# A state tile of four n-parts by 32 channels, and sums that begin with y in PSUM

## The chip, the cores and the metric

The kernel runs on one NeuronCore of one Trainium2 chip. The metric is device time in microseconds; the time before is the median of three runs, 29361.2 us (29357.19 to 29361.32). All data are float32.

## The reference, cut to what matters

The program is four vision layers, one after the other, each of the Mamba kind. Per image (8 of them, 64 x 64 positions, 96 channels) a layer projects to 192 inner channels, convolves, and then scans the positions in K directions (K is 4 in three layers and 1 in the last). For each direction k:

```
x_dbl = einsum('bkdl,kcd->bkcl', xs, x_proj_w)
dts, Bs, Cs = jnp.split(x_dbl, [DT_RANK, DT_RANK + D_STATE], axis=2)
delta = softplus(einsum('bkrl,kdr->bkdl', dts, dt_proj_w) + dt_proj_b)
def step(h, inp):
    dA = jnp.exp(d_t[..., None] * A[None])
    h = dA * h + (d_t * u_t)[..., None] * b_t[:, :, None, :]
    y = jnp.einsum('bkdn,bkn->bkd', h, c_t)
    return (h, y)
ys = scan(step) + Ds * xs
y  = sum of ys over the directions, each put back to its positions
```

With 192 channels d and 16 states n there are 3072 recurrences of 4096 steps for each direction and image. Afterwards y is normalised (in three layers), gated by silu(z), projected to 96 channels and added to x.

## The kernel before, in words

A loop over the 8 images holds the four layers. A layer has a first part (norm, input projection, convolution), the scans, and a last part (norm of y, gates, output projection). The scans take nearly all of the time. They walk over chunks of 512 positions: 8 chunks a direction, in the order of directions 0, 2, 1, 3; directions 2 and 3 run backwards. In all there are 832 chunks.

The work on one chunk, `i`, is cut into 24 *units*; a unit is 128 recurrences over 512 positions. In the kernel before, the 128 partitions of a unit are 2 n-parts by 64 channels (so 3 channel groups t times 8 states j). Four units with the same t make a *state tile* h of 128 x 2048. Six state tiles are a chunk.

For each unit and tile:

- `enter` (matmuls at L942): TensorE forms the input of two units (dbu) in a PSUM tile of two banks. It multiplies du (delta times u, with positions on the partitions, 64 columns of channels) by a block of diagonal matrices with the values of B. 16 products of 64 x 64 weights by 128 columns fill it; each float32 product appears as two records in the trace. There are two such tiles, so TensorE works one tile ahead.
- `decay` (L959): ScalarE forms exp(delta x A) for one unit, four units ahead of the scan. Six buffers.
- `scan` (L973): VectorE runs the recurrence over 512 positions for one unit.
- `keep` (L987): ScalarE copies the last column of the four units as the next chunk's initial state.
- `read_out` (L992): GpSimd multiplies the state tile by C, in place. C stands in SBUF as tiles c of 128 x 2048, two a chunk, each filled by four transfers that repeat rows of DRAM over 64 partitions (`spread_c`, L815). The very last state tile of a layer is done by VectorE (L996).
- `add_up` (L1010): TensorE adds over n with a 0/1 matrix of 64 columns; the sums gather in two PSUM banks (y0 and y1 tiles, `ps_y`).
- `close_sums` (L1019 to L1038): VectorE adds the bank to y in SBUF (L1038), at the places where the direction has its positions; in direction 0 it writes D times u plus the bank (L1032), and ScalarE copies one half (L1036).

The order on every engine is the program's: `tc.manual_schedule` keeps each engine's queue as written. The main loop at L1119 goes over units m; `slot` is m modulo 24 within a chunk. At each m it issues keep and read_out of the tile that was finished (every fourth m), then `enter` for the next pair, `scan(m)`, `decay(m + 4)`, `add_up` (at every fourth slot, for units 15 slots back), and then what the dictionary `plan` (L1041) has for the slot. The plan prepares chunk i + 1, and i + 2:

- v = projection of x_dbl (`turn_v`, L832) at slots 21 and 0; `keep_b` and four steps of softplus on ScalarE at slots 1 to 3; `delta_of` (L877, the sum that ends softplus, on GpSimd) at slot 3.
- `turn_u` (transposes, L849 and L853) at 4 and 5, `du_of` (L880, VectorE) at 7.
- `turn_back` (L898 to L910, delta with the channels back on the partitions) at 8 and 9, and `keep_delta` (L912) at 9, 10, 11: ScalarE copies 64 channels from PSUM into one half of a tile (L917), and a transfer on SP's queue copies them to the other half (L918).
- loads of u (`load_u`, 128 partitions at L749, 64 at L751), x_dbl, `spread_b` and the diagonals (L888, L896), the projection to x_dbl (L765) with `keep_x_dbl` at 18 (L781, then transfers at L790, L792, L794).

All transfers are issued on SP's queue, in the program's order. v, u_t, delta_ps and x_dbl share one PSUM tile of two banks in turn.

Of the kernel before, what the change touches and what calls it, by code (L numbers as in the profile page):

```python
# [30 lines left out]
DI = 192  # L31
NS = 16
NT = 3
NJ = 8
NH = 4
# [10 lines left out]
NEGMEAN, CEN_B, ONE, EPS, N_CONST = 352, 416, 480, 481, 482  # L46
# [73 lines left out]
def kernel(ctx: ExitStack, tc: tile.TileContext, x_in, const_in, *rest):  # L120
# [3 lines left out]
    def pool(name, bufs, space=None):  # L124
# [9 lines left out]
        cpool=pool("c", 3),  # L134
        upool=pool("u", 4),
        deltas=pool("delta", 6),
# [40 lines left out]
def layer(tc, env, x, stats, x_of, x_to, n, ly):  # L177
# [23 lines left out]
    def piece(name):  # L201
        return env.deltas.tile([128, CH], F32, tag="delta", name=name)
# [12 lines left out]
    d = env.wts.tile([128, 2], F32, tag="d", name=f"d{n}")  # L215

    def fold():
        of = win_x[:, 0:by_pe].unsqueeze(1).to_broadcast([C, ly.taps, by_pe])
        nc.vector.tensor_tensor(taps, taps, of, ALU.mult)  # L219

        for o, np_ in enumerate((128, 64)):
            at = ly.d + o * K
            nc.vector.tensor_reduce(
                d[0:np_, o : o + 1], w[0:np_, at : at + K], mybir.AxisListType.X, ALU.add
            )

# [156 lines left out]
    def two_banks(name):  # L383
# [3 lines left out]
        tc, env, n, ly, w, u_mem, u_chunk, d, neg_a, make_ys, two_banks, wide  # L387
# [144 lines left out]
    with set_of("natural_log_exp_and_others"):  # L532
# [15 lines left out]
        env.cpool.tile([128, 4, CH], F32, tag="c", name="gates"),  # L548
# [147 lines left out]
def scans(tc, env, n, ly, w, u_mem, u_first, d, neg_a, make_ys, two_banks, wide):  # L696
# [9 lines left out]
    sel = const[:, SEL : SEL + 64]  # L706
# [3 lines left out]
    RS, SL = 6, 24  # L710
    halves = [slice(0, 64), slice(64, 128)]
# [14 lines left out]

    def place(s):

        i, r = divmod(s, RS)
        return i, r // NT, r % NT  # L730
# [7 lines left out]
    def u_of(i, half):  # L738
        return u_first(half, 0) if i == 0 else us[i][0 : (128, 64)[half], half, :]

    def load_u(i, part):
        if i >= len(walk):
            return
        k, c = walk[i]
        if part == 0:
            us[i] = env.upool.tile([128, 2, CH], F32, tag="u", name="u")
        s = slice(c * CH, (c + 1) * CH)
        if part == 0:
            nc.sync.dma_start(us[i][:, 0, :], u_mem[k % 2][0:128, s])  # L749
        else:  # L750
            nc.sync.dma_start(us[i][halves[part - 1], 1, :], u_mem[k % 2][128:DI, s])  # L751

    def project(i, half):
# [8 lines left out]
        for e in range(2):  # L762
            rows = slice(0, 128) if half == 0 else halves[e if i > 1 else 0]
            u = u_first(half, walk[i][1]) if i < 2 else us[i][rows, half, :]
# [8 lines left out]
    def keep_x_dbl(i):  # L773
# [14 lines left out]
        if i > 1:  # L788
            there = env.deltas.tile([128, CH], F32, tag="delta", name="x_hi")[64 : 64 + XP]
# [17 lines left out]
    def spread_c(i, g, part):  # L807
        k, c = walk[i]
        if part == 0:
            cs[i, g] = env.cpool.tile([128, NH, CH], F32, tag="c", name="c")  # L810
        half, pair = divmod(part, 2)
        rows, js = slice(64 * half, 64 * half + 64), slice(2 * pair, 2 * pair + 2)
        n0 = half * NJ + g * NH + 2 * pair
        of = c_mem[k][n0 : n0 + 2, c * CH : (c + 1) * CH]
        nc.sync.dma_start(cs[i, g][rows, js], of.partition_broadcast(64))  # L815
# [5 lines left out]
    def turn_v(i, b):  # L821


        if b == 0:
            for name in ("delta_t", "du_t"):
                turned[i, name] = env.turned.tile([128, NB4, DI], F32, tag=name, name=name)
# [13 lines left out]
    def turn_u(i, b, half):  # L840
# [5 lines left out]
        for b_ in (b, 2 + b):  # L846
# [3 lines left out]
            else:  # L850
                at = halves[b_ // 2 if i > 0 else 0]
                u = us[i][at, 1, :] if i > 0 else u_of(i, 1)
                nc.tensor.transpose(to[:, 128:DI], block(b_, u), ident[at, at])  # L853

    def softplus(i, part):

        v = turned[i, "v"][:, :, 0:DI]
        if part == 0:
            rests[i] = env.turned.tile([128, NB4, DI], F32, tag="rest", name="rest", bufs=1)
# [38 lines left out]
    def turn_back(i, o, part):  # L898
# [3 lines left out]
        for b in (2 * part, 2 * part + 1):  # L902
            of = turned[i, "delta_t"][:, b]
            for half in range(o + 1 if i == 0 else 1):
                to = deltas[i, "ps"][64 * half : 64 * half + 128 // (o + 1), o]
                of_ = of[:, 0:128] if o == 0 else of[:, 128:DI]
                if half == 0:
                    nc.tensor.transpose(block(b, to), of_, ident)  # L908
                else:
                    nc.tensor.matmul(block(b, to), of_, ident, start=True, stop=True)  # L910

    def keep_delta(i, t):  # L912

        delta = env.deltas.tile([128, CH], F32, tag="delta", name="delta")
        if i > 0:
            here = halves[t % 2]
            nc.scalar.copy(delta[here], deltas[i, "ps"][here, t // 2])  # L917
            nc.sync.dma_start(delta[halves[1 - t % 2]], delta[here])  # L918
        elif t == 2:
            nc.scalar.copy(delta, deltas[i, "ps"][:, 1])  # L920
        else:
            for half in range(2):
                of = deltas[i, "ps"][64 * t : 64 * t + 64, 0]
                nc.scalar.copy(delta[64 * half : 64 * half + 64], of)
        deltas[i, t] = delta


    def enter(q):
# [4 lines left out]
        i, g, t = place(s)  # L933
# [3 lines left out]
        for b in range(NB4):  # L937
            for e in range(2):
                rows = slice(64 * e, 64 * e + 64)
                for half in range(2):  # L940
                    at = b * NS + g * NJ + half * NH + 2 * pair
                    nc.tensor.matmul(  # L942
                        to[64 * half : 64 * half + 64, e, b],
                        du[rows, b, 64 * t : 64 * t + 64],
# [6 lines left out]
    def decay(m):  # L951
# [4 lines left out]
        i, g, t = place(s)  # L956
        d_a = env.decays.tile([128, CH], F32, tag="d_a", name="d_a")
        at = (walk[i][0] * NT + t) * NJ + g * NH + m4
        nc.scalar.activation(d_a, deltas[i, t], AF.Exp, scale=neg_a[:, at : at + 1])  # L959
        decays[m] = d_a  # L960

    def scan(m):
        s, m4 = divmod(m, NH)
        i, g, t = place(s)
# [6 lines left out]
        j = t * NJ + g * NH + m4  # L971
# [268 lines left out]
```

## Time and profile before

| | before |
|---|---|
| median of three runs | 29361.2 us |
| the profiled execution, its own time | 29331.35 us |
| its span | 29329.6 us |
| mean granted TensorE clock | 0.98 |
| VectorE scans, L973 (two groups) | 20778.0 + 2838.3 us busy, 19968 instructions |
| GpSimd products, L992 | 22450.1 us busy, 4960 instructions |
| TensorE dbu, L942 | 11236.9 us busy, 319488 records |
| TensorE sums, L1010 | 9697.2 us busy, 39936 records |
| ScalarE decays, L959 | 13372.2 us busy, 19968 instructions |
| data moved | 3498.19 MB, 119 GB/s |

A group of the page gives the busy time of all its instructions together (overlaps counted once), the mean duration of one, and the idle time of the engine just before them with what ended it. TensorE's records overlap heavily, since different parts of its array work at the same time; for it the time from one group's start to the next in the timeline is the measure, not the duration of one record. A timeline line gives start, length, engine, line, operation and how many instructions were merged; a bracket gives the idle time ahead of it and who ended it.

### The profile page before, as it was taken

To read this page: it belongs to the slowest core of one execution; us is meant where nothing else is said; L and a number is where in the kernel's file an instruction comes from. 1 tells how busy PE (TensorE), PEld (TensorE's weight loads), DVE (VectorE), ACT (ScalarE), POOL (GpSimd) and SP (SyncE) were. 2 spreads that over 40 slices of the span, in tenths; PEclk is the share of its full clock that TensorE was granted. 3 is DMA by queue.
4 is the path that set the end of the run, shared out by engine and by line. 5 is a ranking of instruction groups with operands and counts; after the bars stand their busy time and mean duration, and the time that the engine had idled before them with its cause. 6 is when DMAs were issued, how large, how long until landed. Compare 5 with 4: busy or idle time off the path is not lost. (4 is left out here: it accounts for less than half of the span.)

```text
span 29329.6 us, 919486 instructions
## 1 busy us (share of the span) xinstructions
PE 27127.0 (92%) x391056; PEld 15249.2 (52%) x391056; DVE 27395.8 (93%) x26841; ACT 19839.6 (68%) x35728; POOL 25414.1 (87%) x7101
## 2 busy tenths in 40 slices
PE   9999999999999999999999999999999999999999
PEld 5555455554555545555455554555545555455554
DVE  9999899998999989999899998999989999899998
ACT  6667666676666766667666676666766667666676
POOL 8898788987889878898788987889878898788987
PEclk9999999999999999999999999999999999999999
DMA  5444454454544545445454454544545455454454
GB/s 132 117 117 125 106 131 117 117 125 106 131 116 118 125 107 130 118 118 125 106 132 117 116 126 107 131 117 116 125 106 131 116 117 125 106 132 117 116 126 106
DMA packets 1947780, 3498.19 MB, mean 119 GB/s; under 512 B 448400, under 2 KB 469264, under 8 KB 1920624
## 3 DMA queue, kind: packets, MB, share of 16 engines
q1 hardware_dynamic: 1943664, 3438.91, 47.7%
q8 instruction: 3120, 51.12, 0.8%
q14 instruction: 996, 8.16, 0.1%
HBM read 2787.17 MB, written 302.84 MB: 105 GB/s over the span
## 5 line engine op out<-in xcount | busy, mean ns | idle before, releaser
L992 POOL TENSOR_TENSOR h<-h,c 128x2048 f32<-128x2048 f32 x4960 | 22450.1, 4567 | 44.5 <-ACT state L987 37.6
L973 DVE TENSOR_TENSOR_SCAN h<-d_a,state,dbu 128x512 f32<-128x512 f32 x17472 | 20778.0, 1274 | 13.0 <-PE dbu L942 6.0
L959 ACT ACTIVATE d_a<-delta,neg_a 128x512 f32<-128x512 f32 x19968 | 13372.2, 719 | 428.1 <-DVE h L973 390.9
L942 PE MATMUL dbu<-diag,du_t 64*64 64x128 f32 x319488 | 11236.9, 275 | 1631.8 <-DVE h L973 1606.6
L942 PEld LDWEIGHTS dbu<-diag,du_t 64*64 64x64 f32 x319488 | 8881.1, 131 | 6556.5 <-issue 5591.6
L1010 PE MATMUL y_ps<-h,const 128*64 128x512 f32 x39936 | 9697.2, 605 | 13.3 <-POOL h L992 13.3
L1010 PEld LDWEIGHTS y_ps<-h,const 128*64 128x64 f32 x39936 | 2441.1, 136 | 3802.9 <-issue 3757.3
L987 ACT COPY state<-h 128x4 f32<-128x4 f32 x4992 | 974.6, 195 | 3692.8 <-DVE h L973 3687.3
L973 DVE TENSOR_TENSOR_SCAN h<-d_a,dbu 128x512 f32<-128x512 f32 x2496 | 2838.3, 1201 | 348.9 <-PE dbu L942 227.6
L877 POOL TENSOR_TENSOR delta_t<-delta_t,rest 128x768 f32<-128x768 f32 x832 | 1525.5, 1834 | 1835.3 <-ACT state L987 1508.3
L917 ACT COPY delta<-delta_ps 64x512 f32<-64x512 f32 x2400 | 1392.3, 580 | 1716.2 <-PE delta_ps L908 1677.1
L832 PE MATMUL v<-w,x_dbl 39*128 39x208 f32 (+1 forms) x5120 | 1388.4, 475 | 33.3 <-ACT x_dbl L781 33.3
L480 POOL TENSOR_TENSOR acc<-acc,more 128x512 f32<-128x512 f32 x576 | 757.4, 1317 | 758.0 <-ACT more L479 724.4
L343 PE MATMUL one_bank<-xn,taps 96*128 96x512 f32 (+1 forms) x2496 | 1220.2, 675 | 22.0 <-DVE taps L219 22.0
L832 PEld LDWEIGHTS v<-w,x_dbl 39*128 39x128 f32 (+1 forms) x5120 | 964.1, 317 | 348.4 <-issue 228.9
L880 DVE TENSOR_TENSOR du_t<-delta_t,u_t 128x768 f32<-128x768 f32 x832 | 782.9, 941 | 162.2 <-POOL delta_t L877 162.2
L871 ACT COPY bt<-v 128x64 f32<-128x64 f32 x832 | 176.5, 212 | 1109.7 <-PE v L832 1108.3
L908 PE MATMUL delta_ps<-const,delta_t 128*128 128x128 f32 (+1 forms) x6656 | 925.6, 280 | 0.0
L1038 DVE TENSOR_TENSOR y<-y,y_ps 128x128 f32<-128x128 f32 (+2 forms) x2048 | 843.9, 457 | 52.0 <-PE y_ps L1010 52.0
L621 POOL TENSOR_TENSOR y<-y,rstd 128x512 f32<-128x512 f32 x192 | 244.3, 1273 | 743.6 <-DVE y L624 531.6
L849 PE MATMUL u_t<-const,u 128*128 128x128 f32 x3328 | 850.3, 338 | 0.0
L343 PEld LDWEIGHTS one_bank<-xn,taps 96*128 96x128 f32 (+1 forms) x2496 | 473.7, 205 | 705.4 <-issue 691.5
(109 smaller groups left out, 15376.3 us busy)
## 6 DMA issues: line engine op xcount, KB each, us to landing
c<-cm SPq DMA_DIRECT2D x3584, 256.0 KB
c<-xm SPq DMA_DIRECT2D x3072, 256.0 KB
diag<-rows SPq DMA_DIRECT2D x6656, 64.0 KB
delta<-delta SPq DMA_DIRECT2D x2400, 128.0 KB
u<-u SPq DMA_DIRECT2D x1088, 256.0 KB
u<-u SPq DMA_DIRECT2D x1920, 128.0 KB
u<-u SPq DMA_DIRECT2D x48, 1024.0 KB
x_dbl<-xm SPq DMA_DIRECT2D x512, 78.0 KB
```

What stands on the lines that cost most here:

```text
L343: nc.tensor.matmul(part, taps[:, t, d0 : d0 + nd], rhs, start=t == 0, stop=t == ly.taps - 1)
L832: nc.tensor.matmul(turned[i, "v"][:, 2 * e + b], block(2 * e + b, of), w[o : o + XP, at : at + DI + NS], start=True, stop=True,)
L849: nc.tensor.transpose(to[:, 0:128], block(b_, u_of(i, 0)), ident)
L877: nc.gpsimd.tensor_tensor(delta_t, delta_t, rests.pop(i), ALU.add)
L908: nc.tensor.transpose(block(b, to), of_, ident)
L917: nc.scalar.copy(delta[here], deltas[i, "ps"][here, t // 2])
L942: nc.tensor.matmul(to[64 * half : 64 * half + 64, e, b], du[rows, b, 64 * t : 64 * t + 64], diag[rows, :, at : at + 2], start=True, stop=True,
L959: nc.scalar.activation(d_a, deltas[i, t], AF.Exp, scale=neg_a[:, at : at + 1])
L973: nc.vector.tensor_tensor_scan(hs[s][:, m4, flow], decays.pop(m)[:, flow], p[:, flow], 0.0 if first else states[i // NCH][:, j : j + 1], A ...
L987: nc.scalar.copy(states[i // NCH][:, at : at + NH], hs[s][:, :, last])
L992: nc.gpsimd.tensor_tensor(hs[s], hs[s], cs[i, g], ALU.mult)
L1010: nc.tensor.matmul(sums[i][o][64 * half : 64 * half + 64], sel, hs[of][:, state, :], start=g == 0 and e in (0, 4), stop=g == 1 and e in (3 ...
```

## The change

A unit's 128 partitions become 4 n-parts by 32 channels: six channel groups t times four states j, again 24 units. A state tile holds two t by two j (`groups` gives the order of the six tiles). What follows from it:

- `enter`: 32 products of 64 x 32 weights by 128 columns fill a dbu tile, where 16 of 64 x 64 did; a product's output goes to 32 partitions.
- `add_up`: a 0/1 matrix of 32 columns (`SEL_Q`); four products side by side fill the 128 partitions of a bank.
- delta is needed in all four n-parts. ScalarE copies it from PSUM in two pieces (`keep_delta`), it is written to DRAM, and eight transfers (`spread_delta`) bring it into two tiles of 3 channel groups each, repeated over the four parts.
- C: one tile a chunk, filled by four transfers (repeated over 32 partitions); `read_out` reads it twice, by a repeated row.
- y: `open_sums` begins a bank with a TensorE product: the identity times y so far, or in direction 0 the diagonal of D times u (`diag_d`, made once a layer). `add_up` accumulates onto it, and in `close_sums` ScalarE copies the whole bank to y. VectorE has no part in it any more.
- Buffers: c 2 (3 before), u 3 in two tags (4), delta 4 of 6 KB (6 of 2 KB), one buffer `passing` for the softplus rest, for delta on its way to DRAM and for x_hi. One of the gate tiles of the last part moves from c's buffers to h's.
- The plan: opening at slots 12 and 0, closing at 5 and 13 (11 and 14 before), loads of u at 6, 9, 10 (1, 2, 4 before).

The core of the diff:

```diff
-NT = 3
-NJ = 8
+NQ = 4
+DQ = 32
+NT = DI // DQ
+NJ = NS // NQ
...
-    def keep_delta(i, t):
-
-        delta = env.deltas.tile([128, CH], F32, tag="delta", name="delta")
-        if i > 0:
-            here = halves[t % 2]
-            nc.scalar.copy(delta[here], deltas[i, "ps"][here, t // 2])
-            nc.sync.dma_start(delta[halves[1 - t % 2]], delta[here])
...
+    def keep_delta(i, o):
+
+        if o == 0:
+            deltas[i, "sb"] = passing("delta_sb").rearrange("p (o l) -> p o l", o=2)
+            deltas[i, "mem"] = env.dram.tile([DI, CH], F32, tag="delta", name=f"delta{i}_{n}", bufs=2)
+        rows = slice(0, 128 // (o + 1))
+        nc.scalar.copy(deltas[i, "sb"][rows, o], deltas[i, "ps"][rows, o])
+        at = slice(0, 128) if o == 0 else slice(128, DI)
+        nc.sync.dma_start(deltas[i, "mem"][at], deltas[i, "sb"][rows, o])
+
+    def spread_delta(i, part, q):
+
+        if q == 0:
+            deltas[i, part] = env.deltas.tile([128, 3, CH], F32, tag="delta", name="delta")
+        of = deltas[i, "mem"].rearrange("(t r) l -> r t l", r=DQ)[:, 3 * part : 3 * part + 3]
+        nc.sync.dma_start(deltas[i, part][DQ * q : DQ * q + DQ], of)
...
         for b in range(NB4):
             for e in range(2):
                 rows = slice(64 * e, 64 * e + 64)
-                for half in range(2):
-                    at = b * NS + g * NJ + half * NH + 2 * pair
+                for q_ in range(NQ):
+                    at = b * NS + q_ * NJ + 2 * pair_j
                     nc.tensor.matmul(
-                        to[64 * half : 64 * half + 64, e, b],
-                        du[rows, b, 64 * t : 64 * t + 64],
+                        to[DQ * q_ : DQ * q_ + DQ, e, b],
+                        du[rows, b, at_d : at_d + DQ],
                         diag[rows, :, at : at + 2],
...
-            nc.gpsimd.tensor_tensor(hs[s], hs[s], cs[i, g], ALU.mult)
+            h = hs[s].rearrange("p (t j) l -> p t (j l)", j=2)
+            c = c.rearrange("p j l -> p (j l)").unsqueeze(1).to_broadcast([128, 2, 2 * CH])
+            nc.gpsimd.tensor_tensor(h, h, c, ALU.mult)
...
+    def open_sums(i, o):
+
+        sums[i, o] = env.ps_y.tile([128, CH], F32, tag=f"y{o}", name=f"y{o}_ps")
+        if walk[i][0] == 0:
+            work = [(sums[i, o], us[i, o])]
+        else:
+            work = list(y_pieces(i, o))
+        weights = diag_d[:, o] if walk[i][0] == 0 else ident
+        for at, (to, of) in enumerate(work):
+            nc.tensor.matmul(
+                to, weights, of, start=at == 0, stop=False, skip_group_check=True
+            )
+
+    def close_sums(i, o):
+        for of, there in y_pieces(i, o):
+            nc.scalar.copy(there, of)
...
-        11: [(keep_delta, 1, 2), (close_sums, -1, 0)],
-        14: [(close_sums, -1, 1)],
+        12: [(open_sums, 0, 0)],
+        13: [(close_sums, -1, 1)],
...
-        *((5 + 3 * part, (spread_c, 0, part)) for part in range(4)),
-        *((18 + 3 * part, (spread_c, 1, part)) for part in range(4)),
+        *((12 + q, (spread_delta, 0, q)) for q in range(NQ)),
+        *((17 + q, (spread_delta, 1, q)) for q in range(NQ)),
+        *((8 + 5 * q, (spread_c, q)) for q in range(NQ)),
```

## The prediction

> **What bounds the kernel now.** I first read the page's busy shares: three engines are near full, so shares decide nothing.
>
> ```profile
> PE 27127.0 (92%) x391056; PEld 15249.2 (52%) x391056; DVE 27395.8 (93%) x26841; ACT 19839.6 (68%) x35728; POOL 25414.1 (87%) x7101
> ```
>
> Second, busy time by stretch. Nearly all of the span is scan work, and inside it VectorE has no gap, while TensorE and GpSimd have a few per cent.
>
> ```profile
> 500.00:600.00 100.00, 95.58 (x1516) 55.91 (x1520) 99.83 (x91) 70.31 (x129) 96.06 (x24) 1.00 0.54 128
> ```
>
> Columns: stretch, length, busy us of PE, PEld, DVE, ACT, POOL with counts, TensorE clock, DMA share, GB/s. Third, VectorE's timeline over one chunk (24 scans).
>
> ```profile
> 522.30 0.93 DVE L880 TENSOR_TENSOR du_t<-delta_t,u_t 128x768 f32<-128x768 f32 x1
> 523.14 4.79 DVE L973 TENSOR_TENSOR_SCAN h<-d_a,state,dbu 128x512 f32<-128x512 f32 x4
> 527.84 0.67 DVE L1038 TENSOR_TENSOR y<-y,y_ps 128x512 f32<-128x512 f32 x1
> 528.42 3.63 DVE L973 TENSOR_TENSOR_SCAN h<-d_a,state,dbu 128x512 f32<-128x512 f32 x3
> 531.96 0.67 DVE L1038 TENSOR_TENSOR y<-y,y_ps 128x512 f32<-128x512 f32 x1
> 532.53 20.15 DVE L973 TENSOR_TENSOR_SCAN h<-d_a,state,dbu 128x512 f32<-128x512 f32 x17
> 552.60 0.93 DVE L880 TENSOR_TENSOR du_t<-delta_t,u_t 128x768 f32<-128x768 f32 x1
> ```
>
> From du_t to du_t is 30.30 us: 24 scans at 1.18, the du product at 0.84, two y additions at 0.58 from start to start. Nothing is waited for: VectorE is the bound. GpSimd is next:
>
> ```profile
> 496.32 22.65 POOL L992 TENSOR_TENSOR h<-h,c 128x2048 f32<-128x2048 f32 x5
> 520.18 1.84 POOL L877 TENSOR_TENSOR delta_t<-delta_t,rest 128x768 f32<-128x768 f32 x1 [1.21 <-ACT state L987]
> 521.98 13.61 POOL L992 TENSOR_TENSOR h<-h,c 128x2048 f32<-128x2048 f32 x3
> ```
>
> Six products at 4.53 and one addition at 1.80 make 28.98 us a chunk; its one idle time (1.21) stands ahead of the addition, which waits for ScalarE's softplus. The addition ends at 522.02 and VectorE's du_t starts at 522.30: that handover has 0.28 us to spare. TensorE's timeline:
>
> ```profile
> 518.60 1.12 PE L942 MATMUL dbu<-diag,du_t 64*64 64x128 f32 x32
> 521.05 1.11 PE L942 MATMUL dbu<-diag,du_t 64*64 64x128 f32 x32
> 522.09 1.94 PE L1010 MATMUL y_ps<-h,const 128*64 128x512 f32 x8
> 523.96 1.12 PE L942 MATMUL dbu<-diag,du_t 64*64 64x128 f32 x32
> 525.00 1.09 PE L908 MATMUL delta_ps<-const,delta_t 128*128 128x128 f32 x8
> 526.03 1.11 PE L942 MATMUL dbu<-diag,du_t 64*64 64x128 f32 x32
> ```
>
> A dbu group costs 1.05 us to the next start, an add_up group 1.87. A chunk has 12 and 6 of them: 12.6 + 11.2 us, and 4.7 for the rest (v 2 x 0.73, u_t 1.4, delta_ps 1.03, x_dbl 1.67 in half of the chunks): 28.5 of 30.3.
>
> **The change, part by part.** The sum is made against the profiled execution, 29331.35 us (span 29329.6), which is 0.1% below the median of the runs.
>
> *y leaves VectorE.* L1038 (2048 instructions, 843.9 us) and L1032 (640 in four shapes: 140.9 + 139.9 + 59.4 + 55.5 = 395.7) go: 1239.6 us of busy time. From start to start each takes about 0.09 less than its duration (0.67 against 0.58), so 2688 x 0.09 = 242 comes off: **-1000 us**, all on the bound. A chunk's VectorE time becomes 29.1 us. GpSimd, at 28.98, is 0.1 behind it: the gain ends there, and nothing more could come of VectorE.
>
> *ScalarE copies the bank.* Two copies at about 0.50 from start to start (L917's shape of 512 columns has 0.58 duration), or up to four of 128 to 256 columns a bank in the serpentine layer; one of the three keep_delta copies and the k=0 copy at L1036 go. ScalarE goes from 70 to about 73% and hides it. The copies stand at slots 5 and 13, after ScalarE's rush of softplus (slots 1 to 3) and before its work for delta_ps. Behind each wait decays that run four scans (4.7 us) ahead; the add_up they wait for was issued two slots earlier. Cost 0; without the cover 1.0 a chunk.
>
> *open_sums.* Two 128x128 products by 512 columns a chunk. The nearest row is L343 (128 columns of weights, 512 moving: 1133.0 us for 2112 records, 0.54 each, two records a product): 1.07 each, 2.1 a chunk. The serpentine layer has pieces of 128, by L849's row 0.44 for two, so up to 1.8 a bank. Nothing is waited for: y was written a direction earlier, u a chunk earlier.
>
> *add_up.* The same 48 records a chunk, each now on 32 columns of the array, so four stand beside each other where two did. Bounds: 0.93 us a group if four stream at once, 1.87 if only two do. I take 0.93, as two already start within 0.03 us of each other now.
>
> *dbu: the crux.* 64 records a group where 32 were, of half the weight columns, the same 128 moving. What it costs depends on whether eight tiles stream at once. No row shows eight; the rows of four, in narrow windows (each repeats the whole group so far):
>
> ```profile
> 506.13 0.34 PE L942 MATMUL dbu<-diag,du_t 64*64 64x128 f32 x4 [1.23 <-DVE h L973]
> 506.13 0.45 PE L942 MATMUL dbu<-diag,du_t 64*64 64x128 f32 x8 [1.23 <-DVE h L973]
> 506.13 0.56 PE L942 MATMUL dbu<-diag,du_t 64*64 64x128 f32 x12 [1.23 <-DVE h L973]
> 506.10 0.24 PEld L942 LDWEIGHTS dbu<-diag,du_t 64*64 64x64 f32 x8 [1.44 <-issue]
> ```
>
> Windows: 506.13 to .16, .27 to .33, .376 to .432, and .10 to .25 for the weights. Four matmuls start within 0.03 us, then four more each 0.11 us: a round lasts as long as one tile's stream, and issue uses a quarter to a half of it. Eight rounds of eight then take what eight rounds of four take: 1.05 us. Bounds: 1.05 (eight at once), 2.09 (33 ns a record as now). I take 1.05, since the rounds are paced by the stream. TensorE's chunk is then 12.6 + 5.6 + 2.1 + 4.7 = 25.0 us, under VectorE's 29.1. TensorE becomes the bound from (29.1 - 12.4)/12 = 1.39 us a group, and the kernel slower than before from 1.49.
>
> The Trainium skill speaks against this. "TensorE: Matmul & The Clock Gate", the section "Wait — 56ns, not 53.3ns?", says that matmul starts never come closer than about 25 ns, however few columns. By it a group is 64 x 25 = 1.6 us, a chunk 31.6, the kernel about 30400. "Runtime: NRT & Kernel Launch", section "Instruction fetch mechanics", has a floor of some 20 cycles an instruction, which would be worse. The four starts within 30 ns contradict the first page here; whether 64 can follow each other so, no run here shows.
>
> *delta through memory.* Before: three copies, three transfers of 128 KB between halves (L918). After: two copies, two writes, eight reads of 192 KB for a chunk; SP issues 7 more there, and 4 fewer of c. SP takes 0.5 to 0.6 us an issue (L918 0.51, L815 0.59). First copy at 526.1 by ScalarE's rows, write issued at 526.7, first read after the write's landing. No row gives a landing; the loads of x issued at 1051.18 let POOL L565 start at 1057.42, 6.2 us for two of 768 KB, the upper bound; rows<-bt at 1165.66 lets the diagonals go at 1167.12, 1.5 us, the lower. With 3: reads are issued 530 to 535 among diagonals and c, the last there near 539. Decay 24 wants it at slot 20, about 537.5, its scan comes at 542: a wait on ScalarE that VectorE doesn't see. The second part, behind keep_x_dbl on SP (537.5), ends near 545, for a decay at slot 2 about 546. If late, softplus behind it on ScalarE, then GpSimd's addition, then du_t are, and that handover has 0.28 us. I allow 0.1 to 0.2 us a chunk over 832: **+120 us**; bounds 0 and 1 us a chunk (+830).
>
> *Beside these.* GpSimd's product reads c with a repeated row: I take 4.53 us; bounds 4.5 (the shortest L992) and 4.8 (L480's 1317 ns for 512 columns, times four, would be 5.3, but that holds four starts). Layer ends: add_up is TensorE's tail there (22 records from 1055.24 in 5.4 us); half of three groups, 1.4 us for 32 layers, **-45 us**. Layer starts: 3 copies fewer of 0.58 on ScalarE, against a trip through memory, 0 with 2 us either way, 60 in all. Two diagonals of D per layer: 64 x about 0.3 = **+20 us**. Fewer buffers (c 2, u 3, delta 4): each is refilled after its last reader by at least four slots; 0.
>
> Sum: 29331 - 1000 + 120 - 45 + 20 = 28426; with the 30 us to the median, **28450**, 3.1% faster.
>
> **The rivals.**
> - *TensorE becomes the bound (slower).* More than 1.49 us a dbu group. Halfway between the bounds, at 1.57: chunk 12 x 1.57 + 12.4 = 31.2, +0.9 x 832 = 30150; at 1.65: 32.2, 30900; at 2.09: 37.5, 35300. For: no row with eight tiles, 128 instructions to issue in 1.05 us. Against: the four starts in 0.03 us.
> - *GpSimd takes over.* Its product may grow by 0.02 us without harm; by 0.1, chunk 29.6, 28850; by 0.22 the gain is gone, 29400. For: 96 of 100 us busy; against: same elements, contiguous runs of 1024.
> - *Delta is late.* 0.5 to 1 us a chunk: 28750 to 29150. For: the 0.28 us handover. Against: decays lead by four scans.
> - *The freed time is worth nothing*, another wait filling it to the same time: 29360. VectorE's 99.8% speaks against it.
>
> **How the numbers follow.** Forecast 0.55; TensorE 0.24 (up to 1.65 us a group 0.15, above 0.09); GpSimd 0.09 (0.045 faster, 0.015 the same, 0.03 slower); delta late 0.09; nothing 0.03. Faster 0.55 + 0.09 + 0.045 = 0.68, same 0.03 + 0.015 = 0.05, slower 0.24 + 0.03 = 0.27. By 0.2% a measurement of this kernel can be told from no change. The likeliest case alone lies in 28200 to 28950 (no stall and a better tail; 0.6 us a chunk more). The whole range keeps its lower end and reaches to TensorE at 1.65 us a group: 28200 to 30900; 0.09 lie above, less below.
>
> **What would show it.** Right: du_t to du_t at about 29.1 us, a dbu group of 64 at 1.05 us and add_up at 0.93, GpSimd's idle time before delta_t gone. Wrong: VectorE's scans waiting for dbu with a long group (TensorE), du_t waiting for delta_t (GpSimd or late delta), or d_a waiting for a transfer.

## The result, and the profile after

The changed kernel takes 31935.0 us (median of four runs, 31913.7 to 31973.1) against 29361.3 for the kernel before: 1.0878 times as long, 95% interval 1.0859 to 1.0897. The forecast was 28450, with a range up to 30900. The profiled execution took 31973.06 us, its span is 31971.2, the granted TensorE clock 0.929 (before 0.98).

Page of the changed kernel: the busy line, and the queues with their packets and megabytes.

```profile
PE 27460.2 (86%) x715408; PEld 15417.4 (48%) x715408; DVE 26583.0 (83%) x24217; ACT 19973.2 (62%) x37200; POOL 25543.6 (80%) x7101
...
q1 hardware_dynamic: 2204272, 3887.88, 46.7%
q8 instruction: 5648, 92.54, 1.3%
```

No engine is near full any more. VectorE's busy time fell by 813 us, and its share from 93 to 83%. TensorE has 1.8 times as many records as before (391056), and with them its instruction stream, queue q8, has grown: 92.54 MB in 5648 packets are 16 KB each. For each record there is a weight load, 2 x 715408 instructions in all, so a packet brings about 256 of them, of 64 bytes. The page of before has `q8 instruction: 3120, 51.12, 0.8%`.

One row of the view by stretch, the same stretch as was shown of before (length, then busy us of TensorE, its weight loads, VectorE, ScalarE and GpSimd, then clock, DMA share, GB/s):

```profile
500.00:600.00 100.00, 84.20 (x2453) 49.59 (x2434) 84.84 (x74) 59.59 (x112) 87.20 (x21) 0.91 0.52 130
```

VectorE had 99.83 of 100 us here, and now idles for 15. What it waits for stands in the groups and in the list of waits (waiter, what ended the wait, us in total, times, longest):

```profile
L984 DVE TENSOR_TENSOR_SCAN h<-d_a,state,dbu 128x512 f32<-128x512 f32 x17472 | 20834.6, 1259 | 3008.5 <-PE dbu L950 2266.4
L950 PE MATMUL dbu<-diag,du_t 64*32 64x128 f32 x638976 | 13110.3, 284 | 3551.5 <-issue 2445.8
L1007 POOL TENSOR_TENSOR h<-h,c 128x2048 f32<-128x2048 f32 x4960 | 22557.4, 4582 | 754.4 <-issue 453.9
```

```profile
DVE h L984 <- PE dbu L950: 2666.3, 1826, 5.9
PE dbu L950 <- issue: 2445.8, 1946, 4.9
```

The scans wait for dbu, and dbu waits for "issue": nothing that the profile shows holds it back. Before, the idle time ahead of dbu given to issue was 0.2 us in all. TensorE's timeline shows what such a wait is:

```profile
512.91 1.06 PE L1022 MATMUL y_ps<-h,const 128*32 128x512 f32 x8
513.97 1.10 PE L950 MATMUL dbu<-diag,du_t 64*32 64x128 f32 x58
516.13 1.35 PE L950 MATMUL dbu<-diag,du_t 64*32 64x128 f32 x70 [1.05 <-issue]
517.40 1.07 PE L1022 MATMUL y_ps<-h,const 128*32 128x512 f32 x8
519.26 0.93 PE L950 MATMUL dbu<-diag,du_t 64*32 64x128 f32 x49 [0.79 <-DVE h L984]
522.47 0.45 PE L950 MATMUL dbu<-diag,du_t 64*32 64x128 f32 x15 [2.28 <-issue]
522.85 0.80 PE L842 MATMUL v<-w,x_dbl 49*128 49x208 f32 x4
523.58 1.38 PE L950 MATMUL dbu<-diag,du_t 64*32 64x128 f32 x64
524.90 1.93 PE L1022 MATMUL y_ps<-h,const 128*32 128x512 f32 x8
526.76 1.78 PE L950 MATMUL dbu<-diag,du_t 64*32 64x128 f32 x64
```

A group of 64 is broken in the middle, after 58 records and after 49, though it waits for nothing that the profile shows, and goes on 1 to 2.3 us later. In the packets of q8 the stop after 49 ends 1.5 us after a 16 KB piece has landed (packet from 519.60 to 520.94, next product at 522.47), the one after 58 likewise (513.72 to 514.60, 516.13).

The whole trace says the same. Of the 1946 stops ahead of dbu given to issue, 95% end 1.2 to 1.7 us after a piece has landed; of moments picked at random in the span, 9% lie so. And the stops stand where a new piece begins: if TensorE's instructions are counted in order, the 1384 stops over 0.6 us fall, within the work on one image, at one place in every 256 (185 or 186 in the first image, 70 or 71 in the second), with one exception in all eight images.

The last two lines of the timeline show a second cost: after such a stop a sum group takes 1.86 us to the next start instead of 1.0, and a dbu group 1.7 instead of 1.1. By the view by stretch (columns as above) TensorE's clock has fallen to half:

```profile
512.00:515.00 3.00, 3.00 (x129) 1.73 (x116) 3.00 (x4) 1.46 (x4) 3.00 (x1) 1.00 0.86 244
...
524.90:526.70 1.80, 1.80 (x11) 0.20 (x8) 1.80 (x3) 1.10 (x3) 0.80 (x2) 0.50 0.41 93
526.80:528.40 1.60, 1.60 (x68) 1.35 (x64) 1.11 (x1) 0.23 (x1) 1.60 (x1) 0.69 0.02 6
```

VectorE in the same stretch: four scans at a time, then a gap for dbu.

```profile
516.67 4.79 DVE L984 TENSOR_TENSOR_SCAN h<-d_a,state,dbu 128x512 f32<-128x512 f32 x4 [0.50 <-PE dbu L950]
523.11 4.79 DVE L984 TENSOR_TENSOR_SCAN h<-d_a,state,dbu 128x512 f32<-128x512 f32 x4 [1.65 <-PE dbu L950]
528.69 2.45 DVE L984 TENSOR_TENSOR_SCAN h<-d_a,state,dbu 128x512 f32<-128x512 f32 x2 [0.79 <-PE dbu L950]
```

**How fast the pieces come.** The lines of the scans hold 1,701 TensorE instructions a chunk (records and weight loads, 2 x 707,584 / 832), 6.64 pieces. At the forecast's 29.1 us a chunk, one piece is needed every 4.4 us. From the starts of q8's 16 KB packets in the traces:

| kernel | pieces | median interval, us | 10% to 90% | median time of one packet, us |
|---|---|---|---|---|
| before | 3120 | 8.40 | 5.85 to 11.53 | 1.14 |
| after | 5648 | 4.81 | 3.80 to 6.85 | 1.13 |

A packet takes 1.1 us, yet pieces come no closer than 3.3 us, and 1% of the intervals are under 3.46. What fills the rest of the interval the trace doesn't show. The median isn't a rate of supply by itself, since a TensorE that has its instructions in time asks for no more than it uses: run 6 below, which hardly waits for them, has 4.79.

**Theories.** S: TensorE is starved of instructions; their supply is slow because it stands behind the data transfers. D: delta through memory comes late. T: the narrow tiles, or the opening products, are more TensorE work than the sum said. The runs below are each compared with runs of the kernel before on the same chip (29344 to 29363 us).

### The profile page after: what moved, and what is told of

Its sections match the earlier page's. It is cut to its first block, busy times and chain, and to the rows that moved or that the text cites. A ratio compares the mean times of both kernels' runs of the same rounds, so it can differ in the third digit from the quotient of the medians.

```text
span 31971.2 us, 1569774 instructions
## 1 busy us (share of the span) xinstructions
PE 27460.2 (86%) x715408; PEld 15417.4 (48%) x715408; DVE 26583.0 (83%) x24217; ACT 19973.2 (62%) x37200; POOL 25543.6 (80%) x7101
## 3 DMA queue, kind: packets, MB, share of 16 engines
q8 instruction: 5648, 92.54, 1.3%
## 4 chain that ended last, share of the span: by engine, by line
## 5 line engine op out<-in xcount | busy, mean ns | idle before, releaser
L1007 POOL TENSOR_TENSOR h<-h,c 128x2048 f32<-128x2048 f32 x4960 | 22557.4, 4582 | 754.4 <-issue 453.9
L950 PE MATMUL dbu<-diag,du_t 64*32 64x128 f32 x638976 | 13110.3, 284 | 3551.5 <-issue 2445.8
L950 PEld LDWEIGHTS dbu<-diag,du_t 64*32 64x32 f32 x638976 | 9771.0, 108 | 10562.8 <-issue 6363.7
L968 ACT ACTIVATE d_a<-delta,neg_a 128x512 f32<-128x512 f32 x19968 | 13499.4, 722 | 1990.0 <-DMA delta<-delta 932.9
L1022 PE MATMUL y_ps<-h,const 128*32 128x512 f32 x39936 | 5807.4, 638 | 139.1 <-issue 125.3
L923 ACT COPY delta_sb<-delta_ps 128x512 f32<-128x512 f32 (+1 forms) x1664 | 958.2, 578 | 1349.4 <-PE delta_ps L915 1301.2
L842 PE MATMUL v<-w,x_dbl 39*128 39x208 f32 (+1 forms) x5120 | 1532.6, 507 | 150.1 <-issue 59.7
L1022 PEld LDWEIGHTS y_ps<-h,const 128*32 128x32 f32 x39936 | 835.3, 111 | 1355.2 <-issue 1224.4
L1053 PE MATMUL y_ps<-y,const 128*128 128x128 f32 (+2 forms) x4096 | 1451.7, 473 | 12.0 <-ACT y L1059 5.8
L1059 ACT COPY y<-y_ps 128x512 f32<-128x512 f32 (+2 forms) x2688 | 1028.5, 430 | 120.5 <-PE y_ps L1022 119.0
L776 PE MATMUL x_dbl<-u,w 64*103 64x256 f32 (+3 forms) x3584 | 808.1, 409 | 52.7 <-ACT u L325 29.5
```

What stands on the lines that cost most here:

```text
L842: nc.tensor.matmul(turned[i, "v"][:, 2 * e + b], block(2 * e + b, of), w[o : o + XP, at : at + DI + NS], start=True, stop=True,)
L923: nc.scalar.copy(deltas[i, "sb"][rows, o], deltas[i, "ps"][rows, o])
L950: nc.tensor.matmul(to[DQ * q_ : DQ * q_ + DQ, e, b], du[rows, b, at_d : at_d + DQ], diag[rows, :, at : at + 2], start=True, stop=True,)
L968: nc.scalar.activation(d_a, deltas[i, t // 3][:, t % 3], AF.Exp, scale=neg_a[:, at : at + 1])
L1007: nc.gpsimd.tensor_tensor(h, h, c, ALU.mult)
L1022: nc.tensor.matmul(sums[i, o][DQ * at : DQ * at + DQ], sel, hs[of][:, unit, :], start=False, stop=e in (3, 5), skip_group_check=True,)
```

## The experiments

**1. Half the dbu instructions, all else as changed.**

```
-                for q_ in range(NQ):
+                for q_ in (0, 2):
                     at = b * NS + q_ * NJ + 2 * pair_j
+                    at_64 = min(at_d, DI - 64)
...
-                        to[DQ * q_ : DQ * q_ + DQ, e, b],
-                        du[rows, b, at_d : at_d + DQ],
+                        to[DQ * q_ : DQ * q_ + 64, e, b],
+                        du[rows, b, at_64 : at_64 + 64],
```

> The changed kernel, but dbu in 16 products of 64 x 64 (two channel groups at once, so half of the values are wrong) in place of 32 of 64 x 32: the instructions of before for dbu, the same columns streamed, everything else as changed. Theory S (TensorE's instructions don't arrive fast enough: it stops in the middle of groups for nothing that the trace shows, and what is fetched for it grew from 51 to 93 MB): its idle time put down to issue falls from 2446 us to under 400 and the time to 28300 to 29200 us. Theory D (delta through DRAM is late: ScalarE waits 932.9 us for it and scans wait for ScalarE): stays at 31000 or more. Theory T (TensorE has too much work, the opening products among it): 30500 to 31900, since its streaming is the same.

Measured: 28733.8 us, 0.979 (0.9762 to 0.9819). Its VectorE timeline:

```profile
516.17 0.93 DVE L890 TENSOR_TENSOR du_t<-delta_t,u_t 128x768 f32<-128x768 f32 x1
517.01 28.22 DVE L985 TENSOR_TENSOR_SCAN h<-d_a,state,dbu 128x512 f32<-128x512 f32 x24
545.14 0.94 DVE L890 TENSOR_TENSOR du_t<-delta_t,u_t 128x768 f32<-128x768 f32 x1
```

From du_t to du_t it is 28.97 us, the forecast's chunk, and idle time of dbu given to issue falls to 237.4 us. All of the change but the number and the width of the dbu products is in this kernel (opening, copies, sums of 32 columns, delta through memory, fewer buffers), so what costs is in those products; whether their number or their width, runs 5, 6 and 9 tell.

**2. Decays that don't read delta.**

```
-            d_a, deltas[i, t // 3][:, t % 3], AF.Exp, scale=neg_a[:, at : at + 1]
+            d_a.rearrange("p (o l) -> p o l", o=2),
+            const[:, 0 : CH // 2].unsqueeze(1).to_broadcast([128, 2, CH // 2]),
+            AF.Exp,
+            scale=neg_a[:, at : at + 1]
```

> The changed kernel with every transfer of delta still issued, but the decays computed from a constant tile, so ScalarE never waits for delta (the values of the decays are wrong). Theory S: 31300 to 31900, TensorE's issue idle time about as before (2200 to 2600). Theory D: 29500 or less. If both take part: 30000 to 31000.

Measured: 31958.7 us, 1.0889 (1.0858 to 1.0921), with `PE dbu L950 <- issue` at 2431.1 us. Against the changed kernel nothing changed (the time is 59 us above the range that S had named). The 932.9 us that ScalarE waits for delta there cost nothing; D falls.

**3. C spread once a layer.**

```
+        if i > 0:
+            cs[i] = cs[0]
+            return
         if q == 0:
             cs[i] = env.cpool.tile([128, NJ, CH], F32, tag="c", name="c")
```

> The changed kernel with C spread only for the first chunk of a layer and reused (later chunks use the wrong C): 4 of its 29 or so transfers a chunk go, about 1 of 4.8 MB. Theory S, if the fetches queue behind the data transfers: 29800 to 31200, issue idle of TensorE down by a third or more. Theory S, if a fetch takes as long whatever else is moved: 31700 to 32000. Theory D: 30500 to 31500, since delta lands earlier.

Measured: 29626.6 us, 1.0095 (1.0065 to 1.0124), 2300 us less than the changed kernel. 3149 MB are moved in all where 3989 were, and TensorE's records are all there:

```profile
L953 PE MATMUL dbu<-diag,du_t 64*32 64x128 f32 x638976 | 12583.4, 276 | 2515.4 <-issue 1380.9 <-DVE h L987 990.8 <-PE y_ps L1025 21.8
```

The median interval of the pieces is 4.50 us. With less data TensorE waits 1065 us less for its instructions, and the gain in time is a little more than S had said.

**4. Four-part tiles alone, y as before on VectorE.** The opening products and ScalarE's copies are taken out again, and `close_sums` is the earlier one.

> The four-part tiles alone: y is added by VectorE as before the change, no opening products and no ScalarE copies. Theory S: 31600 to 32600, since hardly any instructions go (4 to 16 records of some 1700 a chunk) and VectorE gets 1.0 ms back that it has idle time for. Theory T: 30000 to 31000, TensorE being relieved of 2.1 us a chunk. Theory D: about 31900.

Measured: 32516.2 us, 1.1079 (1.1047 to 1.1111); issue 2174.1 us. The stops come with the four-part tiles. The y part, on top of them, gains 581 us (32516 - 31935).

**5. The old tiles with as many instructions.** The kernel before, each dbu product cut in two.

```
+                    for o in (0, 32):
                         nc.tensor.matmul(
-                            to[64 * half : 64 * half + 64, e, b],
+                            to[64 * half : 64 * half + 64, e, b, o : o + 32],
                             du[rows, b, 64 * t : 64 * t + 64],
-                            diag[rows, :, at : at + 2],
+                            diag[rows, o : o + 32, at : at + 2],
```

> The kernel before with each dbu product of 128 columns cut into two of 64 columns (the same two-part 64x64 tiles, the same columns streamed, the same transfers, nothing of four-part tiles, nothing of the y part): TensorE's dbu instructions go from 768 to 1536 a chunk, as many as in the changed kernel. Instruction supply (S): TensorE starves as in the changed kernel, 31000 to 33000 us, with over 1500 us of TensorE's idle time before dbu given to issue. Rival (the 64x32 tiles themselves are at fault, in start cost or clock): no starving, 29300 to 30000 us.

Measured: 32334.9 us, 1.1017 (1.0995 to 1.1039), and in its groups

```profile
L974 DVE TENSOR_TENSOR_SCAN h<-d_a,state,dbu 128x512 f32<-128x512 f32 x17472 | 21093.8, 1262 | 2257.9 <-PE dbu L943 1718.2 <-ACT d_a L960 254.2 <-ACT state L988 182.7
L943 PE MATMUL dbu<-diag,du_t 64*64 64x64 f32 x638976 | 13550.4, 225 | 1878.2 <-issue 1027.5 <-DVE h L974 823.0 <-PE dbu L943 4.2
```

The time is S's, the idle time given to issue (1027.5) is below the 1500 that S named: a part of the loss is something else. The timeline names it: a group of 64 half-length products takes 1.25 us to the next start, one of 32 whole ones 1.05.

```profile
528.38 1.31 PE L943 MATMUL dbu<-diag,du_t 64*64 64x64 f32 x64
529.63 0.80 PE L832 MATMUL v<-w,x_dbl 49*128 49x208 f32 x4
530.36 0.48 PE L943 MATMUL dbu<-diag,du_t 64*64 64x64 f32 x16
531.80 1.04 PE L943 MATMUL dbu<-diag,du_t 64*64 64x64 f32 x48 [0.96 <-issue]
```

**6. The same with less data**, to part the two: run 5 with C spread once a layer.

> The kernel before with its dbu products cut in two (1536 dbu instructions a chunk) and with C spread for a layer's first chunk only, which takes some 1.7 GB of the 3.4 GB of transfers away (the values of C in later chunks are those of the first). The doubled products alone took 32335 us. Their groups take 1.25 us on the chip where the uncut ones take 1.05, so TensorE has 28.5 + 12 x 0.2 = 30.9 us a chunk against VectorE's 30.3: 29850 us if nothing else were wrong. S (TensorE waits for its instructions, which queue behind data): 29700 to 30500 us. Rival (the products' length and start cost make the whole loss): 32000 to 32400 us, for their length is untouched.

Measured: 30589.8 us, 1.0417 (1.0397 to 1.0438), 1745 us less than run 5 with the same products. Idle time of dbu given to issue is 60.1 us, the clock 0.979 as before. It ends 90 us above S's range and far below the rival's. So 1745 of run 5's 2980 us go when the instructions are in time: TensorE idles 967 us less for issue, and its busy time is 734 us shorter (29806.3 to 29072.5). The other 1230 stay. By the expectation's sum the longer groups make some 490 of them; the remaining 740 aren't explained (TensorE is busy for 95% of this run). With tiles, sums and y as before, doubling the number of instructions is enough to starve TensorE.

**7. Control: the kernel before with less data.** C spread once a layer there too.

> The kernel before with C spread for a layer's first chunk only (1.7 of 3.4 GB of transfers gone; C of later chunks is that of the first). It is the control for the runs with less data. S (less data speeds the changed kernel because its instructions arrive sooner): before has its instructions in time and VectorE sets its 30.3 us a chunk, so nothing changes, 29200 to 29400 us. Rival (transfers slow the engines or the loads in any kernel, and less data is a gain of its own): under 28900 us.

Measured: 29350.0 us, 0.9997 (0.9987 to 1.0008), with 1819 MB moved instead of 3498. Less data is worth nothing to a kernel that has its instructions in time. That kernel waits for hardly any transfer, though, so the control can't by itself rule out that runs 3 and 6 gained by earlier data. Their lists of waits speak for the supply: from the changed kernel to run 3 the scans wait 1946 us less for dbu (2666.3 to 720.6) and 152 us less for decays (689.4 to 537.1), from run 5 to run 6 1388 us less for dbu (2111.4 to 723.5) and 309 us less for decays (472.9 to 163.8).

**8. More data.** A second spread of C goes into a spare piece of memory, on the changed kernel and on the kernel before (there for half of its spreads, so that both get the same 873 MB more).

```
         nc.sync.dma_start(cs[i][DQ * q : DQ * q + DQ], of.partition_broadcast(DQ))
+        nc.sync.dma_start(spare[0][DQ * q : DQ * q + DQ, :, 0:CH], of.partition_broadcast(DQ))
```

> The changed kernel with the spread of C issued a second time, into a spare piece of memory that nobody reads (same 2 KB rows, some 840 MB more over the run, four more issues a chunk on SP's queue; TensorE's instructions unchanged). S with the supply queueing behind data: the opposite of the run that spreads C once a layer, so about 2300 us more than the changed kernel, 33000 to 35500 us, the interval between instruction pieces longer. If supply has a rate of its own that data does not touch: 31900 to 32200 us.

> The kernel before, with half of its spreads of C issued a second time into a spare piece of memory that nobody reads: 870 MB more, as the same doubling put on the changed kernel, where it cost 2000 us. S: before, TensorE asks for a piece of instructions only every 8.4 us, far above what a piece takes, so more data costs nearly nothing: 29300 to 29700 us. Rival (more transfers slow the engines themselves or the loads they wait for, whatever the instructions): 30500 us or more.

Measured: the changed kernel 33956.9 us, 1.157 (1.1546 to 1.1593), issue 2994.7 us; the kernel before 31057.1 us, 1.0577 (1.0555 to 1.0598). The first is as S said. The second is not: 1700 us, though dbu waited for issue for only 72.1 us. The list of waits of that run shows another mechanism:

```profile
DVE h L978 <- PE dbu L947: 1471.2, 1195, 29.2
PEld v L837 <- DMA x_hi<-x_dbl: 312.9, 240, 7.4
PE v L837 <- DMA x_dbl<-xm: 274.5, 279, 3.3
PE v L837 <- DMA x_hi<-x_dbl: 242.5, 192, 7.1
```

TensorE's projection v waits for x_dbl, which comes late on the crowded queue, and dbu stands behind v in TensorE's order. The waits of v itself for x_dbl are 517 us (274.5 + 242.5); TensorE's busy time is 986 us longer too (28113.1, at a clock of 0.96). How these make up the 1700 us wasn't tested. More data therefore harms in two ways, and of the 2000 us of the changed kernel only a part is instructions (its dbu idle for issue rose by 549 us). Only the runs that take data away bear on S.

**9. Full instructions, little data.** The changed kernel, with C once a layer and delta not moved at all.

```
-        nc.sync.dma_start(deltas[i, "mem"][at], deltas[i, "sb"][rows, o])
...
-        nc.sync.dma_start(deltas[i, part][DQ * q : DQ * q + DQ], of)
+        return
```

> The changed kernel with all of TensorE's instructions, its four-part tiles and its y part as they are, but C spread for a layer's first chunk only and delta neither written to memory nor spread (the decays read a constant tile of the same size): about half of the data transfers are gone. S: supply keeps up, and the rest of the forecast's sum shows: VectorE 29.1 and GpSimd 29.0 us a chunk, 28500 to 29200 us, TensorE's dbu idle given to issue under 700 us (C once alone: 29627 us and 1381 us). Rival (TensorE's work with the narrow tiles is longer than the sum said): no better than 29500 us.

Measured: 28606.3 us, 0.9742 (0.9722 to 0.9761). Busy line, the stretch of before, and TensorE's main group:

```profile
PE 26173.8 (92%) x715408; PEld 14886.2 (52%) x715408; DVE 26438.9 (92%) x24217; ACT 19940.9 (70%) x37200; POOL 25574.8 (89%) x7101
```

```profile
500.00:600.00 100.00, 96.45 (x2919) 57.80 (x2916) 98.18 (x86) 74.22 (x138) 98.77 (x25) 1.00 0.17 47
```

```profile
L947 PE MATMUL dbu<-diag,du_t 64*32 64x128 f32 x638976 | 12546.3, 274 | 1745.9 <-DVE h L984 859.1 <-issue 728.4 <-PE y_ps L1022 45.9
```

The same 715408 records as in the changed kernel, narrow tiles, opening products and copies included, and it is within 160 us of the forecast, with GpSimd and VectorE near full. (The decays read a constant tile in this run; run 2 has shown that this alone changes nothing in the time of the changed kernel.) Issue is a little over the 700 us that was named. T falls: TensorE has time for this work if its instructions are there. Against the changed kernel TensorE idles 1717 us less for issue (2445.8 to 728.4) and its busy time is 1286 us shorter (27460.2 to 26173.8, the clock 0.976 instead of 0.929); the two make 3003 of the 3329 us between the runs.

**10. Longer rows.** The bytes of the changed kernel, but C and delta lie in memory so that their spreads read 8 KB and 6 KB in a piece.

> The changed kernel with the same bytes moved in longer rows: C lies in memory chunk by chunk, so that its spread reads 8 KB in one piece where it read four of 2 KB, and delta lies so that its spread reads 6 KB where it read three of 2 KB (four more issues a chunk on SP's queue for the write). Nothing else changes. If the instructions wait for a number of queued data packets: the supply quickens, 30000 to 31300 us. If they wait for bytes: 31700 to 32100 us; and if a longer packet in front is a longer wait: above 32100 us.

Measured: 32885.3 us, 1.1215 (1.1195 to 1.1235).

```profile
L970 ACT ACTIVATE d_a<-delta,neg_a 128x512 f32<-128x512 f32 x19968 | 13436.4, 720 | 3814.7 <-DMA delta<-delta 1813.2 <-DMA diag<-rows 1009.6 <-DMA x_hi<-x_dbl 663.4
L952 PE MATMUL dbu<-diag,du_t 64*32 64x128 f32 x638976 | 13359.0, 288 | 2832.5 <-issue 1601.3 <-DVE h L986 987.1 <-DMA diag<-rows 76.3
```

The data packets are 1512048 where they were 2204272. The time lies where "a longer packet is a longer wait" had put it, but the rows don't show that reason: the pieces of instructions come about as before (median 4.87 us), dbu waits less for issue (1601.3 us against 2445.8), and delta, the diagonals and x_dbl come later. Whether bytes or packets hold the instructions back stays open.

**11. The y part alone.** On the kernel before, for directions 1 to 3: both banks, or the second only, the latter with the opening at slot 17 and at slot 20.

```
+            nc.tensor.matmul(to, ident, of, start=at == 0, stop=False, skip_group_check=True)
...
+            elif begun(i, o):
+                nc.scalar.copy(there, of)
             else:
                 nc.vector.tensor_tensor(there, there, of, ALU.add)
```

> The kernel before (two-part tiles) with only the y part of the change, on the three directions that add to y (directions with k > 0, 640 of 832 chunks); the first direction stays on VectorE. Adds about 12 instructions a chunk to TensorE, so no starving is expected. TensorE gets 2.1 us more on 28.5 a chunk (30.6), VectorE 1.4 us less than its 30.3. TensorE becomes the bound of these chunks by 0.3 us: 29300 to 29900 us. If the y part alone were what costs (rival to S): over 30500 us.

> As y1, but only the second of the two y banks is begun by TensorE and copied by ScalarE; the first stays on VectorE. TensorE 28.5 + 1.05 = 29.55 us a chunk, VectorE 30.3 - 0.7 = 29.6: the two balance. 0.5 to 0.7 us of gain on 640 chunks: 28800 to 29150 us, faster than both kernels, with TensorE's idle time before dbu given to issue under 100 us. If freed VectorE time were worth nothing: 29350 us.

> The kernel before with only the second y bank begun by TensorE and copied by ScalarE, as in the run of one bank, but the opening product issued three slots later, away from the projection that it followed there and that made ScalarE late (VectorE waited 332 us for decays in that run, against 94 before). VectorE then keeps its 0.7 us on 640 chunks less what TensorE, at 29.55 us a chunk, can't follow: 28950 to 29200 us, faster than both kernels. If TensorE is already the bound at 29.55 us or more: 29300 to 29400 us.

Measured: both banks 29416.1 us, 1.0021 (1.0011 to 1.0031); the second at slot 17 29383.8 us, 1.0012 (1.0002 to 1.0021); at slot 20 29606.6 us, 1.0082 (1.0065 to 1.0099). With one bank VectorE's busy time did fall by 322 us (27395.8 to 27073.9), and its scans waited nearly as much longer: 331.6 us for decays (93.8 before) and 299.5 for dbu (233.6). Moving the opening away from the projection brought the decays back to 188.7 us and raised the wait for dbu to 574.0. The first is as expected, and far from the 30500 us of its rival: the y part alone is not what costs. The two expectations of a gain missed, and the last run is slower than its own rival said too. That TensorE, at 94% busy and in a fixed order, can't give dbu in time any more is how we read it; it wasn't tested further. By this reading the y part needs the room that the narrow sums make.

No version that computes the reference beat the kernel before; runs 1 and 9, which are faster, leave out work that the result needs.

**The runs side by side.** Instructions of dbu are records and weight loads, in thousands; the third column is all that was moved.

| run | dbu instr. | MB | dbu idle, issue | clock | time |
|---|---|---|---|---|---|
| before | 639 | 3498 | 0.2 | 0.98 | 29361 |
| 7 before, C once | 639 | 1819 | none listed | 0.981 | 29350 |
| 1 changed, half the dbu products | 639 | 3948 | 237 | 0.968 | 28734 |
| after | 1278 | 3989 | 2446 | 0.929 | 31935 |
| 3 changed, C once | 1278 | 3149 | 1381 | 0.964 | 29627 |
| 9 changed, C once, no delta | 1278 | 1512 | 728 | 0.976 | 28606 |
| 5 before, products cut | 1278 | 3539 | 1028 | 0.965 | 32335 |
| 6 the same, C once | 1278 | 1860 | 60 | 0.979 | 30590 |

Either half of the instructions or a good part of the data has to go for TensorE to be fed.

## Why the prediction was wrong, point by point

- *y leaves VectorE*: right. The forecast was -1000 us; its busy time fell by 813 us in the changed kernel and by 1020 in run 1, where TensorE was fed (27395.8 to 26375.8) and the chunk shown took 28.97 us against 29.1 forecast. On top of the four-part tiles the y part was worth 581 us in a kernel that starved (run 4).
- *ScalarE copies the bank*: forecast 0, and no run isolates it. The copies are 1028.5 us busy. The scans wait 271.7 us for decays in run 1 and 381.2 in run 9, against 93.8 before; what part of that the copies have isn't shown.
- *open_sums*: forecast 1.07 us each; `529.20 1.12` of the changed kernel's timeline is a bank of two records, about 1.05 to the next start. Right.
- *add_up*: forecast 0.93 a group where four products stand side by side, measured 1.00 to 1.06 between starts where nothing stopped it (503.17 to 504.17, 512.91 to 513.97). Right, a little short; nearer to four at once than its other bound of 1.87.
- *dbu: the crux*: the step that failed. Eight tiles do stream at once, a fed group of 64 takes 1.09 us (from 504.17 to the next at 505.26; forecast 1.05). The failing sentence was "issue uses a quarter to a half of it": it took what can be issued within a group for what can be issued for ever. The bounds, 1.05 and 2.09, were of a group with its instructions at hand, and left out what brings them: 6.64 pieces a chunk, one each 4.4 us, where beside this kernel's data they came at a median of 4.81. Against the forecast's sum of 28426 the span is 3545 us longer, 4.26 a chunk; 2.94 of that is dbu's idle time for issue (2445.8 / 832), and TensorE's slower clock adds 1.55 of busy time against run 9 (1286 / 832), some of which lies in gaps that others leave, for the two together are more than the 4.26. Of the Trainium skill's rules weighed there, that of "TensorE: Matmul & The Clock Gate", section "Wait — 56ns, not 53.3ns?" (about 25 ns between starts at least, by which a group was estimated at 1.6 us), is contradicted by 64 records in 1.09 us, 17 ns each. "Runtime: NRT & Kernel Launch", section "Instruction fetch mechanics", had the right object: instructions come in 16 KiB blocks of 256, as q8 shows. It calls the cost of crossing a block mostly hidden, and here it was not.
- *delta through memory*: forecast +120 us. Run 2 shows no cost in this kernel: ScalarE does wait for delta (932.9 us), under a longer wait. What it costs a kernel whose TensorE is fed no run isolates. Run 1, which has it, is 278 us above the sum in its profiled execution (28703.63), with 237.4 us of waiting for issue among them, which leaves no room for +830.
- *Beside these*: GpSimd's product was taken as 4.53 us from start to start; its mean duration went from 4567 to 4582 ns, so the repeated row costs next to nothing. That GpSimd stands close behind VectorE was right: in 500 to 600 us of run 1 it is busy for 99.90 us, VectorE for 99.49. The diagonals of D took 18.3 us (forecast 20). The shorter layer ends (-45) no run isolates.
- *Rivals*: "TensorE becomes the bound" had the right engine and sign, and the wrong mechanism: by its price, the time of 31935 would mean groups of 1.75 us, and the groups are 1.09 with stops between them. Its "for" named the cause, 128 instructions in 1.05 us, and priced it as group length.

## What to carry to other kernels

Where a change multiplies the instructions of an engine, count them per unit of time: here TensorE was starved at some 1,700 instructions in 29 us beside 125 GB/s of data, and nearly fed at about half of that, or beside 53 GB/s (237 and 728 us of waiting left). An idle time that the profile gives to "issue" in the middle of a run of like instructions, while q8 has grown, is the sign of it; that such stops end a fixed time after a packet of q8 has landed, here some 1.5 us, is the test. Finer tiles that save array time were paid for twice here, in waits and in the lower clock that came after them; products of the same columns in fewer instructions, or less data beside them, are what helped.

## What the runs showed of the hardware that was not expected

- The instructions of TensorE come in 16 KB pieces whose packets take 1.1 us, and yet follow each other no closer than 3.3 us in the changed kernel. When TensorE stops for one, it goes on 1.2 to 1.7 us after the piece has landed.
- Their supply slows with data traffic: 3989, 3149 and 1512 MB beside the same instructions gave 2446, 1381 and 728 us of waiting. Whether it is the bytes, the packets or something else in the traffic is open (run 10).
- Some 2 us after the end of the 2.28 us stop shown, the granted clock went to 0.50 for 3.4 us (a sum group then took 1.86 us instead of 1.0). In the whole trace such a spell begins within 5 us of the start of a stop given to issue for 85% of the 420 stops over 2 us and for 40% of the 451 between 1.2 and 2 us, and within 5 us of 12% of moments picked at random. The changed kernel has 758 spells, the one before 120; over the run the clock was 0.929, against 0.976 in run 9. That stops bring it down is how we read this order; no run tests it.
- Cutting a product of 64x64 by 128 columns into two of 64 columns costs 0.2 us on 1.05 in a group, though the columns are the same.
